# A third of seven block products split into seven: the experts' first layer of a gated cross-attention block

## The chip, the cores and the metric

The kernel runs on one core of a Trainium2 chip. A core has five engines that run their own instruction queues and meet through semaphores: TensorE (PE; matmuls, into the eight PSUM banks), VectorE (DVE), ScalarE (ACT), GpSimd (POOL) and SyncE (SP; here it only issues DMAs). Weight loads for TensorE are shown as an engine of their own, PEld. The metric is the device time of one execution in microseconds (us). Everything is float32; a matmul instruction of the program appears in the trace as two records.

## The reference

A gated block over 4096 tokens of 512 features, with a context of 3202 rows:

```python
x = x + jnp.tanh(g_xattn[0]) * _L0_xattn_ref(_layernorm(x), ctx_1024, w_sim, b_sim, W_qv, b_qv)
x = x + jnp.tanh(g_ffn[0]) * _L0_ffn_ref(_layernorm(x), w_router, b_router, w1, b1, w2, b2)
```

The first part is a cross-attention. The second part, the one that is touched here, is a mixture of 8 experts: each token goes to its two best experts, an expert has 640 places, and

```python
buf = zeros((e, cap, d)).at[e_flat, posc].add(where(keep[:, None], xf[tok], 0.0))     # e=8, cap=640, d=512
h = gelu(einsum('ecd,edf->ecf', buf, w1) + b1[:, None, :], approximate=False)          # f=2048
out = einsum('ecf,efd->ecd', h, w2) + b2[:, None, :]
```

after which the rows are weighted by the gates and added back to their tokens.

## The kernel before

The attention comes first (lines up to about 1600), then routing (`s2`), then one loop over the 8 experts (`for e in range(E)`), which is the part that matters here. An expert takes about 120 us: a first, hidden layer of some 59 us and an output layer of some 61 us.

**The hidden layer.** It works feature-major: `hT[p, l, idx, t]` holds 128 features by 640 tokens per (l, idx). The layer runs over `idx` = 0 to 7, called blocks here; a block makes two groups of 128 features, `lo` (l = 0) and `hi` (l = 1). Its weights are a 2x2 of pieces (two halves of the 512 inputs, lo and hi), its tokens a 2x2 as well (two halves of the inputs, two halves of the 640 tokens, `HC` = 320). So a block is a 2x2 by 2x2 matrix product, and it is done with seven products in place of eight (Strassen in Winograd's form). The sums of the weights come from `w1_sums` (line 1646, VectorE, written into the spare tiles `w1s` or over a piece of the weights), the sums of the tokens from `x_forms` (line 2068). A product (`product`, line 2273, in `hidden`, line 2256) is two matmul instructions, 128 features by 320 tokens, with 256 inputs. The products are numbered as in the code:

- 0 goes to bank X; ScalarE copies X to Y (line 2301)
- 3 goes to bank Q; ScalarE copies Q to `p5` in SBUF (L2305)
- 4 is added onto Y; ScalarE copies Y to Z (L2310)
- 1 is added onto X; ScalarE applies gelu to X: first half of lo (L2315); VectorE: second half of lo is Y + p5 (L2318, or L2332)
- 5 is added onto Z; ScalarE copies Z to the first half of hi, or to bank W (L2327); VectorE: second half of hi is Z + p5 (L2328)
- 6 is added onto Y and 2 onto W, in blocks 6 and 7 alone; elsewhere they are split.

**The split of products 2 and 6.** For two neighbouring blocks, called a pair (0 to 3), the same product of both is a matrix product of 256 features, 256 inputs and 320 tokens, again a 2x2 by 2x2 of pieces (128 x 128 by 128 x 160). For products 2 and 6 of pairs 0 to 2 `parts` (line 2216) does it with seven sub-products of one matmul instruction each, 160 tokens wide, which `hidden` lays between the products of one later block (1 to 6) in three steps (`first`, `second`, `third`). Its operands are made by `deep_w` (L2210 to L2213) and `deep_x` (L2197 to L2200), its partial results lie in a PSUM tile of three slots from the pool `ps_tr` (tag "tr", two tiles used in turn, also by the transposes) and in half a bank, moved on by two small copies (L2234, L2238), and four VectorE additions put them onto `hT` (L2246 to L2249).

**The order.** The order on each engine is written out by hand: `chained(eng, op)` puts an operation behind the last one given for that engine (`mm`, `dv`, `ac`, `ld`). The order of the program is therefore the order of each queue. Gelus whose input is not ready are put on a list, `owed`, and laid in by `due(n)` at given places of the next block. The semaphore waits follow from the data, a PSUM or SBUF tile that is used again waits for the last reader of what it held before. GpSimd does almost nothing here but issue indirect DMAs: five gathers of the output rows at an expert's start (L2435) and five scatters at its end (L2508), the gathers waiting until the scatters of the expert before have landed. Expert 0 has some of its first products done ahead (`early`) and is otherwise alike.

**The output layer** uses the sets of tiles `sets[0]` and `sets[1]`, and `u2` and `p7`, for the operands of its own two-level products (`inner`, `deep`, `plain`); `p5s` and the operands of the hidden layer's split lie in the same tiles while these are free.

Of the kernel before, what the change touches and what calls it, by code (L numbers as in the profile page):

```python
# [9 lines left out]
ALU = mybir.AluOpType  # L10
# [10 lines left out]
def gated_layer(ctx, tc, x, x_t, ctxt, ctxt_t, ctxt_c, ctxt_r, g_xattn, g_ffn, w_sim, w_sim_r, b_sim, W_qv, W_qv_t, b_qv, b_qv_c, w_router, b_router, w1, b1, w2, b2, out):  # L21
# [1974 lines left out]
    with ExitStack() as s3:  # L1996
# [20 lines left out]
        def dv(*ops):  # L2017
            return chained("dv", *ops)

        def ac(*ops):  # L2020
            return chained("ac", *ops)

        def ld(*ops):
            return chained("ld", *ops)
# [149 lines left out]
        def rows_of(ti, s):  # L2174
# [9 lines left out]
            k: (b, [flat_set[i][:, q * HH : (q + 1) * HH] for q in range(3)] + [p7[:, i - 5, :HH]])  # L2184
            for k, i, b in (("2", 5, xT[2]), ("6", 6, B22))
        }

        def w_of(k, pair):
            n = 3 * (2 * (pair % 2) + (k == "6"))
            return [flat_set[2 + (n + q) // 4][:, (n + q) % 4 * P : ((n + q) % 4 + 1) * P] for q in range(3)]  # L2190

        def deep_x(k):

            b, (t1, t2, t4, t3) = x_of[k]
            b11, b12, b21, b22 = (b[:, c, d : d + HH] for c in range(2) for d in (0, HH))
            return [
                lambda: tt(t1, b12, b11, ALU.subtract),  # L2197
                lambda: tt(t2, b22, t1, ALU.subtract),
                lambda: tt(t3, b22, b12, ALU.subtract),
                lambda: tt(t4, b21, t2, ALU.subtract),  # L2200
            ]

        def deep_w(e, k, pair):

            a = w1_forms(e, pair // 2)[int(k)]
            f = pair % 2 * 2 * P
            a11, a12, a21, a22 = (a[:, c, f + r : f + r + P] for r in (0, P) for c in range(2))
            s1, s2, s4 = w_of(k, pair)
            return [
                lambda: tt(s1, a21, a22, ALU.add),  # L2210
                lambda: tt(s2, s1, a11, ALU.subtract),
                lambda: tt(a21, a11, a21, ALU.subtract),
                lambda: tt(s4, a12, s2, ALU.subtract),  # L2213
            ]

        def parts(e, k, pair, c_bank):

            XWQ = ps_tr.tile([P, DC, P], F32, name=f"d{e}_{k}{pair}", tag="tr").rearrange("p c t -> p (c t)")
            X, W, Q = (XWQ[:, i * HH : (i + 1) * HH] for i in range(3))
            YZ = banks[c_bank][:, : 2 * HH]  # L2220
            Y, Z = YZ[:, :HH], YZ[:, HH:]
            a = w1_forms(e, pair // 2)[int(k)]
            f = pair % 2 * 2 * P
            a11, a12, s3, a22 = (a[:, c, f + r : f + r + P] for r in (0, P) for c in range(2))
            s1, s2, s4 = w_of(k, pair)
            b, (t1, t2, t4, t3) = x_of[k]
            b11, _, b21, b22 = (b[:, c, d : d + HH] for c in range(2) for d in (0, HH))
            dst = hT[:, 0, 2 * pair : 2 * pair + 2, HC:] if k == "6" else hT[:, 1, 2 * pair : 2 * pair + 2, :HC]

            def first():  # L2230
                mm(X, a11, b11, True, True)
                mm(Q, s1, t1, False, True)
                mm(W, a22, t4, False, True)
                ac(lambda: nc.scalar.copy(Y, X))  # L2234

            def second():
                mm(Y, s2, t2, False, True)
                ac(lambda: nc.scalar.copy(Z, Y))  # L2238
                mm(X, a12, b21, False, True)

            def third():
                mm(Z, s3, t3, False, True)
                mm(Y, s4, b22, False, True)

            adds = [
                lambda: tt(dst[:, :, HH:], dst[:, :, HH:], Q.unsqueeze(1).to_broadcast([P, 2, HH]), ALU.add),  # L2246
                lambda: tt(dst[:, :, :HH], dst[:, :, :HH], XWQ[:, : 2 * HH].rearrange("p (f t) -> p f t", f=2), ALU.add),
                lambda: tt(dst[:, 0, HH:], dst[:, 0, HH:], Y, ALU.add),
                lambda: tt(  # L2249
                    dst[:, 1, :].rearrange("p (d t) -> p d t", d=2), dst[:, 1, :].rearrange("p (d t) -> p d t", d=2),  # L2250
                    Z.unsqueeze(1).to_broadcast([P, 2, HH]), ALU.add,
                ),
            ]
            return first, second, third, adds, dst

        def hidden(e, idx):

# [11 lines left out]
            if 1 <= idx <= DEEP_IDX:  # L2269
                k, pair = ("6", idx // 2) if idx % 2 else ("2", idx // 2 - 1)  # L2270
                part = parts(e, k, pair, 5 if split else 2 + (idx + 1) % 2)

            def product(ps, k, start=False):
                for i in range(2):
                    mm(ps, A[k][i], XS[{2: 6, 6: 2}.get(k, k)][i], start and i == 0, i == 1)

            def step(i):
                if part:
                    part[i]()

            def due(n):
                ac(*owed[:n])
                del owed[:n]

            if there and idx:
                ac(lambda: nc.scalar.copy(Y, early.pop(f)))  # L2286
                step(0)
                product(Y, 4)
                due(1)
                ac(lambda: nc.scalar.copy(Z, Y))  # L2290
                step(1)
                product(Q, 3, True)
                ac(lambda: nc.scalar.copy(p5, Q))
                step(2)
                due(1)
            else:
                if there:
                    ac(lambda: nc.scalar.copy(Y, early.pop(f)))
                else:
                    product(X, 0, True)  # L2300
                    ac(lambda: nc.scalar.copy(Y, X))
                step(0)
                due(1)
                product(Q, 3, True)
                ac(lambda: nc.scalar.copy(p5, Q))  # L2305
                step(1)
                if not part:
                    due(1)
                product(Y, 4)
                ac(lambda: nc.scalar.copy(Z, Y))  # L2310
                step(2)
                due(1)
            if not there:
                product(X, 1)
                ac(lambda: nc.scalar.activation(lo[:, :HC], X, AF.Gelu, bias=b_lo))  # L2315
            due(len(owed))
            if split:
                dv(lambda: tt(lo[:, HC:], Y, p5, ALU.add))  # L2318
# [108 lines left out]
        for e in range(E):  # L2427
# [2 lines left out]
                ld(lambda: load_w2(e, 0), lambda: load_w2(e, 1))  # L2430
            b2_t = sb.tile([P, D], F32, name=f"b2_{e}", tag="b2", bufs=1)
            ld(lambda: nc.sync.dma_start(b2_t, b2[e].partition_broadcast(P)))
            cf, ti = cf_of[e], ti_of[e]
            for s in range(NST):
                gather = nc.gpsimd.indirect_dma_start(  # L2435
# [12 lines left out]

            (B11w, B12w, B21w, B22w), right, inner = output(e)
            bias = [add(s, slice(None), b2_t) for s in range(NST)]  # L2450
            dv(*deep_w(e, "6", 0), *deep_x("6"))
            if e:
                dv(*w1_sums(e, 0, 2))
            for idx in range(2 * KQ):
                if more and idx == 2:
                    ld(*[lambda s=s: rows_in(e + 1, s) for s in range(NST - 1)])
# [6 lines left out]
                    dv(*deep_w(e, "2", 0), *deep_x("2"))  # L2463
                if idx in (1, 3):
                    dv(*deep_w(e, "6", 1 + idx // 2), *deep_w(e, "2", 1 + idx // 2))
                if idx in (4, 6, 7):
                    k = (0, 2, 4)[(4, 6, 7).index(idx)]
                    dv(left(1, k, k + 2), left(3, k, k + 2))
# [175 lines left out]
```

## Time and profile before

| | us |
|---|---|
| median of 3 runs (2552.12 to 2552.47) | 2552.36 |
| the profiled execution, its own time | 2551.32 |
| its span, first to last instruction | 2549.5 |
| one expert, from a point of the chain to the same point of the next (1630.15 to 1750.20) | 120.05 |
| hidden layer of expert 1 (1704.70 to 1763.50) | 58.80 |
| one product, from starts (four records of 320) | 1.077 |

In the profile's timelines each row has its start and its duration in us, the engine, the source line, the operation, the tiles written and read (buffer numbers left out), the shapes and the number of instructions merged; in brackets is the time that the engine was idle before, and what ended it. All matmuls of the expert stage have line L2027, the helper that issues them; `d` is a PSUM tile of the split, `bank` a bank, `l` a tile of `sets`, `w` and `w1s` weights and their sums. The records of TensorE overlap: their starts are measured, their ends modelled. In a table of stretches the columns are busy time and number of instructions of PE, PEld, DVE, ACT and POOL, then the granted TensorE clock, the DMA share and GB/s.

### The profile page before, as it was taken

To read this page: it belongs to the slowest core of one execution; us is meant where nothing else is said; L and a number is where in the kernel's file an instruction comes from. 1 tells how busy PE (TensorE), PEld (TensorE's weight loads), DVE (VectorE), ACT (ScalarE), POOL (GpSimd) and SP (SyncE) were. 2 spreads that over 40 slices of the span, in tenths; PEclk is the share of its full clock that TensorE was granted. 3 is DMA by queue.
4 is the path that set the end of the run, shared out by engine and by line. 5 is a ranking of instruction groups with operands and counts; after the bars stand their busy time and mean duration, and the time that the engine had idled before them with its cause. 6 is when DMAs were issued, how large, how long until landed. Compare 5 with 4: busy or idle time off the path is not lost.

```text
span 2549.5 us, 37831 instructions
## 1 busy us (share of the span) xinstructions
PE 2531.7 (99%) x14256; PEld 2214.7 (87%) x14256; DVE 1974.8 (77%) x4118; ACT 715.8 (28%) x1556; POOL 275.5 (11%) x399
## 2 busy tenths in 40 slices
PE   9999999999999999999999999999999999999998
PEld 7788888998988988989989887798888888888978
DVE  8887865876967868859658657887888888787877
ACT  1112302323123123123231144424232332424150
POOL 0101220001001000000000056010101010101010
PEclk9999999999999999999999999999999999999999
DMA  7568795875976957758748895322313141414120
GB/s 265 194 215 295 268 350 175 281 266 167 317 226 205 307 194 241 265 188 285 249 154 292 272 353 190 130 100 95 133 67 133 71 156 43 162 42 158 47 103 21
DMA packets 198407, 489.08 MB, mean 192 GB/s; under 512 B 22462, under 2 KB 79102, under 8 KB 196176
## 3 DMA queue, kind: packets, MB, share of 16 engines
q1 hardware_dynamic: 151984, 386.37, 45.0%
q0 software_dynamic: 21696, 59.07, 6.4%
q10 hardware_dynamic: 24544, 41.21, 4.4%
q8 instruction: 113, 1.85, 0.3%
q14 instruction: 70, 0.57, 0.1%
HBM read 397.40 MB, written 97.52 MB: 194 GB/s over the span
## 4 chain that ended last, share of the span: by engine, by line
PE 89%; issue 5%; DVE 4%; POOL 1%; DMA 1%; ACT 0%; POOLq 0%; SPq 0%; DVEq 0%
PE bank L2027 30%; PE bank L761 21%; PE bank L984 13%; PE bank L1153 6%; PE bank L1510 5%; PE x1p L1755 2%; PE bank L1254 2%; PE d L2027 2%; PE p7d L1510 1%; PE p4d L1510 1%; PE bank L813 1%; PE v L1254 1%; PE bps L2103 1%; DVE SM L1023 1%; PE bank L990 1%
## 5 line engine op out<-in xcount | busy, mean ns | idle before, releaser
L761 PE MATMUL bank<-Qp,kt 128*128 128x256 f32 x1344 | 305.2, 379 | 0.0
L761 PEld LDWEIGHTS bank<-Qp,kt 128*128 128x128 f32 x1344 | 254.4, 190 | 34.1
L2027 PE MATMUL bank<-w,hT 128*128 128x256 f32 (+1 forms) x1280 | 260.7, 359 | 0.7 <-ACT u L2519 0.7
L2027 PEld LDWEIGHTS bank<-w,hT 128*128 128x128 f32 x1280 | 223.8, 190 | 27.4 <-ACT u L2519 1.1
L761 PE MATMUL bank<-q,kt 128*128 128x256 f32 x1008 | 231.3, 379 | 0.0
L761 PEld LDWEIGHTS bank<-q,kt 128*128 128x128 f32 x1008 | 191.5, 190 | 26.0
L2027 PE MATMUL bank<-bT,w 128*128 128x320 f32 x736 | 211.1, 432 | 0.6 <-ACT bank L2310 0.6
L984 PE MATMUL bank<-dt,vf 128*128 128x128 f32 x1680 | 204.8, 275 | 0.0
L984 PEld LDWEIGHTS bank<-dt,vf 128*128 128x128 f32 x1680 | 196.0, 192 | 0.0
L2027 PEld LDWEIGHTS bank<-bT,w 128*128 128x128 f32 x736 | 136.6, 190 | 50.5 <-ACT bank L2310 1.1
L2027 PE MATMUL bank<-XT,w1s 128*128 128x320 f32 x512 | 156.4, 433 | 0.1
L804 DVE TENSOR_TENSOR M<-M,E_all 128x1024 f32<-128x1024 f32 x80 | 97.9, 1223 | 46.0 <-ACT E_all L721 44.6
L2508 POOL DMA_INDIRECT out<-acc,ti x40 | 39.7, 992 | 806.7 <-DVE acc L2447 800.0
L1755 PE MATMUL x1p<-W,q2T 128*128 128x264 f32 x512 | 117.7, 391 | 3.0 <-DVE lg L1777 1.8
L717 DVE TENSOR_TENSOR E_all<-bank,p5s 128x512 f32<-128x512 f32 x42 | 28.9, 688 | 113.4 <-ACT bank L716 113.3
L1755 PEld LDWEIGHTS x1p<-W,q2T 128*128 128x128 f32 x512 | 97.7, 192 | 20.1 <-PE pos L1871 1.8
L2027 PEld LDWEIGHTS bank<-XT,w1s 128*128 128x128 f32 x512 | 91.9, 190 | 25.9 <-ACT bank L2286 0.5
L891 DVE TENSOR_TENSOR E_all<-E_all,mb 128x1024 f32<-128x1024 f32 x84 | 101.2, 1211 | 10.3 <-ACT mb L866 10.3
L984 PE MATMUL bank<-E_all,vf 128*128 128x128 f32 x828 | 106.5, 275 | 0.0
L892 ACT ACTIVATE E_all<-E_all 128x1024 f32<-128x1024 f32 x84 | 88.8, 1057 | 49.8 <-DVE E_all L891 49.3
L984 PEld LDWEIGHTS bank<-E_all,vf 128*128 128x128 f32 x828 | 99.8, 192 | 0.3
L2027 PEld LDWEIGHTS bank<-l,l 128*128 128x128 f32 x736 | 92.9, 192 | 7.6
(644 smaller groups left out, 4955.1 us busy)
## 6 DMA issues: line engine op xcount, KB each, us to landing
vf<-vf_d SPq DMA_DIRECT2D x122, 768.0 KB
kt<-kt_d SPq DMA_DIRECT2D x84, 512.0 KB
w<-in_w SPq DMA_DIRECT2D x16, 2048.0 KB
w<-in_w SPq DMA_DIRECT2D x32, 1024.0 KB
kt<-in_ctxt_t SPq DMA_DIRECT2D x84, 384.0 KB
wp<-wt_d SPq DMA_DIRECT2D x56, 520.0 KB
buf_d<-zero SPq DMA_DIRECT2D x80, 129.0 KB
xb<-buf_d SPq DMA_DIRECT2D x39, 258.0 KB
```

The lines of the kernel that those rows point to most:

```text
L717: tt(dst(1, 1), Z, p5, ALU.add)
L761: nc.tensor.matmul(ps[:, jl, :], kts[j][:, KSLOT[p], k, :], B[p][:, k, :], start=start and jl == 0 and k == 0, stop=stop and k == 1, skip_ ...
L804: tt(M, M, e[:, :, h], ALU.max)
L891: live[g]["last"] = tt(e, e, m, ALU.subtract)
L892: live[g]["exp"] = nc.scalar.activation(e, e, AF.Exp)
L984: nc.tensor.matmul(ps, a[:, j, :], rhs[r][:, j, :], start=start and j == 0, stop=j == NP - 1 and (rest is None or add is None), skip_group ...
L1153: nc.tensor.matmul(ps[b], vt[:, j - i * JH, b * P : (b + 1) * P], right(j) if j < NJ else right_c, start=start and j == 0 and b == 0, stop ...
L1254: mm = nc.tensor.matmul(acc[k][:, b, :], a[:, b * P : (b + 1) * P], r, start=start and b == 0, stop=stop, skip_group_check=True,)
L1510: nc.tensor.matmul(ps[m], A[p][:, k, m * P : (m + 1) * P], wt[:, k, :], start=start and k == 0, stop=stop and k == DC - 1, skip_group_chec ...
L1755: mm = nc.tensor.matmul(ps[:, j, :B1], qTs[g][:, c, q * P : (q + 1) * P], W1[:, c, j, :], start=(c == 0), stop=(c == DC - 1))
L2027: return chained("pe", lambda: nc.tensor.matmul(ps, a, b, start=start, stop=stop, skip_group_check=True))
L2508: sc = nc.gpsimd.indirect_dma_start(out=out[:, :], out_offset=rows_of(ti, s), in_=accs[s][:, :], in_offset=None, bounds_check=N - 1, oob_i ...
```

## The change

For pairs 1, 2 and 3 (in expert 0: 2 and 3), product 3 of the two blocks is also split into seven sub-products. In a block where that holds (`triple`), products are issued without product 3 and without its copy to `p5`; in the even block of the pair, `parts(e, "3", ...)` is laid in (`extra`), ahead of the split of products 2 or 6 at each of the three steps. Its results are copied into both `p5s` tiles by three ScalarE copies (`copies`) and completed by two VectorE additions; the odd block then uses the second of them. The steps of the splits move: step 1 comes after product 4 and step 2 after product 1. Of the places where owed gelus are laid in, two are left out in a `triple` block, so that what is owed beyond one comes after the gelu of product 1.

The operands of the new split are made by GpSimd, four sums of 128x160 per expert (`deep_x("3")`) and four of 128x128 per pair (`third_w`), in tiles of `sets[0]` and in `u2`. The first eight of them stand in GpSimd's queue ahead of the expert's gathers; the lines that make VectorE's sums there are moved up with them. The other fours follow blocks 3 and 5.

```diff
+        flat_low = [t.rearrange("p a b -> p (a b)") for t in sets[0]]
+        x_of["3"] = (xT[0], [flat_low[6][:, q * HH : (q + 1) * HH] for q in range(3)] + [u2[:, 0, :HH]])
+
+        def third_split(e, idx):
+            return idx >= (KQ if e == 0 else 2)
 
         def w_of(k, pair):
+            if k == "3":
+                return [flat_low[4 + pair % 2][:, q * P : (q + 1) * P] for q in range(3)]
...
-        def deep_x(k):
+        def deep_x(k, tt=tt):
...
-        def deep_w(e, k, pair):
+        def deep_w(e, k, pair, tt=tt):
...
-            X, W, Q = (XWQ[:, i * HH : (i + 1) * HH] for i in range(3))
+            X, W, Q = (XWQ[:, i * HH : (i + 1) * HH] for i in ((2, 0, 1) if k == "3" else (0, 1, 2)))
...
+            def copies():
+                nc.scalar.copy(p5s[1], XWQ[:, : 2 * HH])
+                nc.scalar.copy(p5s[0][:, :HH], X)
+                return nc.scalar.copy(p5s[0][:, HH:], Q)
+
             adds = [
+                lambda: tt(p5s[0][:, HH:], p5s[0][:, HH:], Y, ALU.add),
+                lambda: tt(
+                    p5s[1].rearrange("p (d t) -> p d t", d=2), p5s[1].rearrange("p (d t) -> p d t", d=2),
+                    Z.unsqueeze(1).to_broadcast([P, 2, HH]), ALU.add,
+                ),
+            ] if k == "3" else [
...
+            triple = third_split(e, idx)
+            extra = parts(e, "3", idx // 2, 1) if triple and idx % 2 == 0 else None
...
             def step(i):
+                if extra:
+                    extra[i]()
                 if part:
                     part[i]()
...
                 step(0)
                 due(1)
-                product(Q, 3, True)
-                ac(lambda: nc.scalar.copy(p5, Q))
-                step(1)
-                if not part:
-                    due(1)
+                if not triple:
+                    product(Q, 3, True)
+                    ac(lambda: nc.scalar.copy(p5, Q))
+                    step(1)
+                    if not part:
+                        due(1)
                 product(Y, 4)
                 ac(lambda: nc.scalar.copy(Z, Y))
-                step(2)
-                due(1)
+                step(1 if triple else 2)
+                if not triple:
+                    due(1)
             if not there:
                 product(X, 1)
                 ac(lambda: nc.scalar.activation(lo[:, :HC], X, AF.Gelu, bias=b_lo))
+            if triple:
+                step(2)
+            if extra:
+                ac(extra[5])
+                dv(*extra[3])
             due(len(owed))
...
+            dv(*deep_w(e, "6", 0), *deep_x("6"))
+            if e:
+                dv(*w1_sums(e, 0, 2))
+
+            def third_w(pair):
+                return chained("gp", *deep_w(e, "3", pair, nc.gpsimd.tensor_tensor))
+
+            chained("gp", *deep_x("3", nc.gpsimd.tensor_tensor))
+            if third_split(e, 2):
+                third_w(1)
             cf, ti = cf_of[e], ti_of[e]
...
-            dv(*deep_w(e, "6", 0), *deep_x("6"))
-            if e:
-                dv(*w1_sums(e, 0, 2))
             for idx in range(2 * KQ):
...
+                if idx in (3, 5):
+                    third_w(1 + idx // 2)
```

More of the change, by code (lines that the diff above doesn't have):

```diff
@@ L2227, in parts @@
             b11, _, b21, b22 = (b[:, c, d : d + HH] for c in range(2) for d in (0, HH))
[L2228 removed]
+            dst = None if k == "3" else hT[:, 0, 2 * pair : 2 * pair + 2, HC:] if k == "6" else hT[:, 1, 2 * pair : 2 * pair + 2, :HC]
             def first():
@@ L2253, in parts @@
             ]
-            return first, second, third, adds, dst
+            return first, second, third, adds, dst, copies
         def hidden(e, idx):
```

## The prediction

> **What bounds the kernel now.** I read the engines' shares and the chain that ended last first, then the stretch table over one hidden layer, then the timelines of TensorE and ScalarE inside it, since the change lies there alone.
>
> ```profile
> PE 2531.7 (99%) x14256; PEld 2214.7 (87%) x14256; DVE 1974.8 (77%) x4118; ACT 715.8 (28%) x1556; POOL 275.5 (11%) x399
> PE 89%; issue 5%; DVE 4%; POOL 1%; DMA 1%; ACT 0%; POOLq 0%; SPq 0%; DVEq 0%
> 1704.70:1763.50 58.80, 58.80 (x262) 44.78 (x261) 42.90 (x113) 30.82 (x75) 7.12 (x7) 1.00 0.44 161
> ```
>
> The third line is expert 1's hidden layer: 58.80 us long, TensorE (the figure after the comma) busy for all of it at clock 1.00, VectorE 42.90, ScalarE 30.82, GpSimd 7.12. TensorE alone is the limit, so time comes only from fewer matmul columns, and goes wherever TensorE is made to wait.
>
> TensorE in blocks 1 to 3:
>
> ```profile
> 1711.18 0.43 PE L2027 MATMUL d<-bT,w1s 128*128 128x160 f32 x2
> ...
> 1715.23 3.39 PE L2027 MATMUL bank<-bT,w 128*128 128x320 f32 x12
> 1718.46 0.43 PE L2027 MATMUL d<-XT,w 128*128 128x160 f32 x2
> 1718.73 0.43 PE L2027 MATMUL d<-l,l 128*128 128x160 f32 x2
> ...
> 1733.03 0.43 PE L2027 MATMUL d<-XT,w 128*128 128x160 f32 x2
> ```
>
> Starts give the true rate, ends are modelled. Twelve records of 320 columns take 1718.46 - 1715.23 = 3.23 us; a product is four, so 1.077 us (its last record is drawn to 1.24). A block takes (1733.03 - 1711.18)/3 = 7.283 us; less five products that leaves 1.90 for its seven sub-products (two records of 160 each): 0.271 each.
>
> Block 7, the last, has no split pair; TensorE, then ScalarE:
>
> ```profile
> 1755.96 1.24 PE L2027 MATMUL bank<-bT,w 128*128 128x320 f32 x4
> 1757.04 2.32 PE L2027 MATMUL bank<-XT,w1s 128*128 128x320 f32 x8
> 1759.19 2.32 PE L2027 MATMUL bank<-bT,w 128*128 128x320 f32 x8
> 1762.42 1.28 PE L2027 MATMUL bank<-XT,w 128*128 128x320 f32 x4
> 1763.54 0.81 PE L2027 MATMUL bank<-w,hT 128*128 128x256 f32 x3
> ```
> ```profile
> 1757.24 0.41 ACT L2301 COPY bank<-bank 128x320 f32<-128x320 f32 x1 [2.82 <-PE bank L2027]
> 1758.69 0.56 ACT L2325 ACTIVATE hT<-hT,b_t 128x320 f32<-128x320 f32 x1
> 1759.72 0.56 ACT L2325 ACTIVATE hT<-hT,b_t 128x320 f32<-128x320 f32 x1
> 1760.47 0.53 ACT L2315 ACTIVATE hT<-bank,b_t 128x320 f32<-128x320 f32 x1 [0.19 <-PE bank L2027]
> 1760.90 0.55 ACT L2335 ACTIVATE hT<-hT,b_t 128x320 f32<-128x320 f32 x1
> 1761.35 0.52 ACT L2336 ACTIVATE hT<-bank,b_t 128x320 f32<-128x320 f32 x1
> 1761.90 0.41 ACT L2327 COPY bank<-bank 128x320 f32<-128x320 f32 x1
> ```
> ```profile
> PEld bank L2027 <- ACT bank L2327: 2.2, 8, 0.3
> 2491.57 0.70 PE L2027 MATMUL bank<-w,hT 128*128 128x256 f32 x2 [0.68 <-ACT u L2519]
> ```
>
> The reader is to see three things. The copy of product 0 starts 0.04 after the product's drawn end (1755.96 + 1.24) and is hidden behind product 3. The copy to W, which product 2 needs, ends at 1762.31, just ahead of product 2 at 1762.42, and the weight loads already wait for it in all 8 experts: block 7 has no slack on ScalarE. And what a bare copy costs: in the last expert TensorE stood idle 0.68 behind a copy that lasts 0.59, so 0.09 more than the copy.
>
> **The change part by part.** The sum is made against the profiled execution's 2551.32 us; the median is 1.04 above it. Pairs of blocks changed: expert 0 two, the seven others three, 23 in all.
>
> Matmuls. Per pair, two products of 1.077 go and seven sub-products of 0.271 come: 2.153 - 1.900 = 0.253 us. Times 23: **-5.8**.
>
> Block 7, first bubble. Without product 3 nothing stands between product 0 and product 4, and product 4 adds onto the copy of product 0. TensorE could go on 1.077 after product 0's start; it may go on at 1.24 + 0.41 + 0.09 = 1.74. Bubble 0.66, times 8 experts: **+5.3**.
>
> Block 7, second bubble. Five activations are owed when it begins. Before, three were laid between the products; now one is, and four stand between the gelu of product 1 (L2315) and the copy to W. From block start: product 4 at 1.74, product 1 at 2.81, its gelu at 2.81 + 1.28 = 4.09; the next activation 0.43 later (1760.47 to 1760.90), the further three 0.45 apart (1760.90 to 1761.35), the copy 0.55 after the last (1761.35 to 1761.90): 6.42; TensorE goes on 0.41 + 0.05 later, 6.88. It wants product 2 at 2.81 + 3 x 1.077 = 6.04. Bubble 0.84, less 0.04 that is lost there already (1763.54 - 1762.42 against 1.077): 0.80, times 8: **+6.4**. The hi addition and later steps follow the W copy as before, so no more is lost behind it.
>
> A buffer that comes free late. An even changed block now takes two of the two PSUM tiles for sub-products, so the next block's split must wait until VectorE has read the even block's own one. Even block, from its start: product 0 to 1.08, two triples of sub-products to 2.70, product 4 to 3.78, four to 4.87, product 1 to 5.94, four to 7.02, product 5 to 8.10; the odd block's first sub-product is wanted at 9.18. ScalarE: gelu of product 1 at 6.14, then the three new copies at 6.57, 6.89 and 7.08 (0.43, 0.32 and 0.19 apart, as 320- and 160-column copies are in the trace), the last done at 7.37. VectorE, which ends block 1's work 4.5 us into block 2 (at 1721.9) and then idles: the two new additions at 7.39 and 7.62, the lo addition at 8.02, the split's first two at 8.42 and 8.82 (0.23 and 0.40 apart, as at 1723.82 and 1722.62), the second done at 9.30; TensorE goes on at 9.34. Wait 0.16, in blocks 3 (seven experts) and 5 (eight): **+2.4**. Block 7 takes no such tile.
>
> GpSimd's sums: 32 of 128x160 and 92 of 128x128. No row shows a two-input sum of this size there. Nearest: a one-input 128x128 operation, 0.295 us; the far end, the 128x512 fill, 0.56. Each queue that they pass: ahead of the gathers stand 8 of them for an expert (4 in the first), but the gathers wait for the scatters to land until 1715.40 anyway, while the scatters were issued by 1706.9: 8 fit at up to 1.0 us. The first user, block 2, is at 1718.46; if an operation took over 1.4 us, TensorE would wait for them. The later two groups of four follow the gathers and are wanted 7 us on; the scatters at the expert's end come after them. So their own time is costed at nothing. What they may cost is VectorE: if the two engines get in each other's way, four operations delay VectorE by 0 to 4 x 0.56. Its additions for block 3's split end 1.19 before block 4 wants that tile, and block 5's 1.0 before block 6. Taking turns at 0.295, 1.18 is lost: 0 in block 4, 0.18 in block 6, times 8: **+1.4**, which I take as the nearest row gives it; ends 0 and, at 0.56, 7 x 1.05 + 8 x 1.24 = 17. A gain is excluded: these sums are new work. At the expert's start VectorE has 2.3 us in hand ahead of block 1's split (its last operand is done at 1708.85 and wanted at 1711.18) against 4 such operations.
>
> The Trainium skill speaks against this part (SBUF — State Buffer, "Who interferes with whom"): a VectorE operation with two SBUF inputs and a GpSimd operation that reads SBUF exclude each other for a whole instruction, and which goes first decides. No row of this trace shows it. GPSIMD Engine Reference ("Elementwise — side-by-side cycle accounting") has 4497 ns for 2048 elements, an estimated 0.28 us for 128: by that four turns cost 1.1 and this term would be 0.8 instead.
>
> Costed at nothing: the two additions a pair on VectorE (0.23 + 0.40 beside 15.9 us that it idles in this layer; their lateness is counted above); three more small ScalarE copies a pair outside block 7 (28 us idle); the moved VectorE sums, which keep their place on that engine because only GpSimd's gathers stood between. If that cover went, TensorE would wait at the next copy, at 0.4 each.
>
> Sum: -5.8 + 5.3 + 6.4 + 2.4 + 1.4 = +9.7: 2561.0 for the profiled execution, **2562** against the median.
>
> **The rivals.**
> The saving comes whole, and the kernel is faster: the mechanism is that block 7's copies stay hidden because they start before the drawn ends, which are modelled. It gives 2552.4 - 5.8 = 2546.6. For it: seven blocks an expert show no wait on such a copy. Against: the 0.68 row is a wait on just such a copy. It decides where both bubbles together are under (5.8 - 2.4)/8 = 0.43 us, against 1.46 here.
> The tile wait and the port cost nothing and the second bubble is half as long (activations closer together when they stand in a row): -5.8 + 5.3 + 3.2 = +2.7, 2555. Against: 0.45 is the spacing of two that do stand in a row.
> VectorE and GpSimd block each other fully: 4 x 0.45 = 1.8 lost per group, 7 x 0.6 + 8 x 0.8 = 10.6 in place of 1.4: 2571. For it: VectorE runs without a gap just where the sums become ready (the S1 sum at 1718.45 and after). Against: it idles 3 us before each block's late additions, where GpSimd can catch up if VectorE goes first.
>
> **How the numbers follow.** No change to be told from noise is within 0.2%, 5.1 us. Forecast 0.65, the whole saving 0.05, the small loss 0.11, the blocked port 0.19. The forecast's own range is 2558 to 2566: the bubbles 0.15 either way per expert (1.2), the tile wait 0 to 0.3 (2.4 down, 2.1 up). The range, 2556 to 2570, cuts about half of the small loss, all of the faster case and the upper part of the blocked port. Faster 0.05, same 0.11, slower 0.84.
>
> **What would show it.** In an expert with three pairs 24 matmul records of 320 columns go and 42 of 160 come. Product 4 of block 7 starts 1.7 after product 0, and its product 2 about 0.8 late behind L2327's copy; in blocks 3 and 5 the first sub-product waits 0.1 to 0.2 for a VectorE addition; GpSimd's sums show 0.3 to 0.5 us each. An expert's period, 120.05 before (1630.15 to 1750.20), should be 121.3. The prediction is wrong if block 7 shows no idle TensorE, or if TensorE waits for GpSimd in block 2.

## The result, and the profile after

The changed kernel takes 2562.8 us in the median (2562.31 to 2563.99, six runs), the kernel before 2552.24 beside it (2551.55 to 2554.75, six runs): a ratio of 1.0044, with a 95% interval of 1.0033 to 1.0054. It is slower by 10.6 us. The profiled execution took 2562.84 us with a span of 2561.1.

The engines' shares and the chain that ended last, after:

```profile
PE 2532.4 (99%) x14394; PEld 2223.6 (87%) x14394; DVE 2006.3 (78%) x4164; ACT 723.8 (28%) x1625; POOL 357.1 (14%) x523
PE 89%; DVE 4%; issue 4%; ACT 1%; POOL 1%; DMA 1%; another core or an unknown queue 0%; POOLq 0%; SPq 0%; DVEq 0%
```

TensorE has 138 records more, 6 for each of the 23 pairs (14 of 160 columns in place of 8 of 320). GpSimd's busy time grew by 82 us, and ScalarE has 1% of the chain where it had 0%. That 1% is block 7. TensorE in block 7 of expert 1, after:

```profile
1760.11 1.24 PE L2027 MATMUL bank<-bT,w 128*128 128x320 f32 x4
1761.85 1.34 PE L2027 MATMUL bank<-XT,w1s 128*128 128x320 f32 x4 [0.50 <-ACT bank L2324]
1763.03 2.32 PE L2027 MATMUL bank<-bT,w 128*128 128x320 f32 x8
1765.19 1.24 PE L2027 MATMUL bank<-bT,w1s 128*128 128x320 f32 x4
1767.10 1.34 PE L2027 MATMUL bank<-XT,w 128*128 128x320 f32 x4 [0.67 <-ACT bank L2357]
1768.28 7.07 PE L2027 MATMUL bank<-w,hT 128*128 128x256 f32 x32
```

Product 4 starts 1.74 after product 0 (1761.85 - 1760.11) instead of 1.077. Product 2 starts 1.91 after product 6 (1767.10 - 1765.19). Behind both waits the product takes 1.18 to the next start (1763.03 - 1761.85, 1768.28 - 1767.10): 0.10 more than one in full flow, and this is drawn as 1.34 instead of 1.24. The queue of ScalarE in the same block:

```profile
1764.31 0.53 ACT L2340 ACTIVATE hT<-bank,b_t 128x320 f32<-128x320 f32 x1 [0.67 <-PE bank L2027]
1764.74 1.00 ACT L2355 ACTIVATE hT<-hT,b_t 128x320 f32<-128x320 f32 x2
1765.64 0.55 ACT L2365 ACTIVATE hT<-hT,b_t 128x320 f32<-128x320 f32 x1
1766.09 0.51 ACT L2366 ACTIVATE hT<-bank,b_t 128x320 f32<-128x320 f32 x1
1766.63 0.41 ACT L2357 COPY bank<-bank 128x320 f32<-128x320 f32 x1
```

The gelu of product 1 (L2340) is followed by four owed activations without a gap, and the copy that product 2 needs (L2357; it was L2327 before) comes only then. Over the whole expert stage the waits of TensorE (total, times, longest) are:

```profile
PE bank L2027 <- ACT bank L2357: 5.4, 8, 0.7
PE bank L2027 <- ACT bank L2324: 4.0, 8, 0.5
PE d L2027 <- DVE l L2204: 2.0, 1, 2.0
```

Eight waits for each of the two copies, one per expert, and one long wait for VectorE in expert 0, which the prediction had not spoken of. Before, TensorE was idle for 0.95 at that place (1595.52, with no releaser named in that profile). Where the prediction had expected the tile wait, in block 3, there is none; TensorE, then VectorE:

```profile
1728.25 2.32 PE L2027 MATMUL bank<-bT,w 128*128 128x320 f32 x8
1730.40 0.43 PE L2027 MATMUL d<-bT,w1s 128*128 128x160 f32 x2
```
```profile
1729.66 0.48 DVE L2264 TENSOR_TENSOR hT<-hT,d 128x320 f32<-128x320 f32 x1
1730.05 0.48 DVE L2265 TENSOR_TENSOR hT<-hT,d 128x320 f32<-128x320 f32 x1
```

The first sub-product starts at 1730.40, exactly two products behind 1728.25 and so without any wait, while the addition that was to hold it up (L2265) still runs until 1730.53.

Below, "stage" is the time from the first sub-product of expert 0's block 1 to the end of the span (before: 2549.5 - 1594.14 = 955.4; after: 2561.1 - 1593.75 = 967.4), and "period" the time from one expert to the next (before 120.05; after 121.25 for the first five experts and 121.00 for the others). The stage grew by 12.0 us.

### The profile page after: what moved, and what is told of

Read it like the earlier page. It is cut to its first block, busy times and chain, and to the rows that moved or that the text cites. A ratio compares the mean times of both kernels' runs of the same rounds, so it can differ in the third digit from the quotient of the medians.

```text
span 2561.1 us, 38523 instructions
## 1 busy us (share of the span) xinstructions
PE 2532.4 (99%) x14394; PEld 2223.6 (87%) x14394; DVE 2006.3 (78%) x4164; ACT 723.8 (28%) x1625; POOL 357.1 (14%) x523
## 4 chain that ended last, share of the span: by engine, by line
PE 89%; DVE 4%; issue 4%; ACT 1%; POOL 1%; DMA 1%; another core or an unknown queue 0%; POOLq 0%; SPq 0%; DVEq 0%
PE bank L2027 30%; PE bank L761 21%; PE bank L984 13%; PE bank L1153 6%; PE bank L1510 5%; PE d L2027 3%; PE bank L1254 2%; PE x1p L1755 2%; PE p7d L1510 1%; PE p4d L1510 1%; PE bank L813 1%; PE v L1254 1%; PE bps L2103 1%; DVE SM L1023 1%; PE bank L990 1%
## 5 line engine op out<-in xcount | busy, mean ns | idle before, releaser
L2027 PE MATMUL bank<-bT,w 128*128 128x320 f32 x736 | 217.3, 432 | 0.6 <-ACT bank L2334 0.6
L2027 PE MATMUL bank<-l,l 128*128 128x128 f32 (+1 forms) x782 | 109.2, 280 | 0.0
L2027 PEld LDWEIGHTS bank<-l,l 128*128 128x128 f32 x782 | 100.7, 192 | 7.8 <-issue 0.4
L2027 PE MATMUL bank<-XT,w1s 128*128 128x320 f32 x328 | 102.7, 440 | 4.1 <-ACT bank L2324 4.0
```

What stands on the lines that cost most here:

```text
L2027: return chained("pe", lambda: nc.tensor.matmul(ps, a, b, start=start, stop=stop, skip_group_check=True))
```

## The experiments

The kernel before runs beside every group of experiments. It took 2551.89 beside the first four and 2545.2 to 2545.6 beside the rest, where the expert stage of the experiments' kernels also begins 6 to 8 us earlier (1588 instead of 1594 to 1596); what a kernel costs is therefore always its distance to the kernel before of the same group. Intervals are 95%.

### Block 7: the two bubbles one by one, and together

The second bubble is undone by laying the owed activations in again: two at step 0 in block 7, and one behind product 4 wherever no split of products 2 and 6 is laid in.

```diff
-                due(1)
+                due(2 if triple and not part else 1)
...
-                if not triple:
+                if not (triple and part):
                     due(1)
```

> Only the places of ScalarE's owed activations in block 7 are changed: two behind the copy of product 0 and one behind the copy of product 4, where one and none were; two are left ahead of the copy to W in place of four. Theory A (the second bubble of block 7 is the order of ScalarE's queue): the wait behind the copy to W goes, 0.83 us and the 0.10 by which the first matmul after a wait is longer, less the 0.04 that the kernel before loses there too, 8 times: -7.1, 2555.7 us. The first bubble (0.66) stays. Theory B (the loss is GpSimd's sums slowing VectorE, and a wait taken away at one place comes back at the next): under 2 us gained, 2561 or more.

Measured: 2555.23 us (2554.01 to 2556.28), 1.0012 of before (1.0003 to 1.0021), +3.3 us. The waits for L2357 are gone, those for L2324 stay at 4.0.

The first bubble is undone by issuing product 0 of block 7, with its copy, already in block 6, ahead of that block's product 2.

```diff
-                else:
+                elif idx < KF - 1:
                     product(X, 0, True)
                     ac(lambda: nc.scalar.copy(Y, X))
...
+                if idx == KF - 2:
+                    for i in range(2):
+                        mm(X, w1_forms(e, h)[0][:, i, (f + 1) * P : (f + 2) * P], XS[0][i], i == 0, i == 1)
+                    ac(lambda: nc.scalar.copy(banks[3][:, :HC], X))
                 product(W, 2)
```

> Only product 0 of block 7 and its copy are moved: ahead of block 6's product 2, so that this product covers the copy. Theory A: the first bubble goes, 0.66 + 0.10, 8 times: -6.1, 2556.7 us; the second bubble stays at 0.83, since ScalarE's queue behind it is the same. Theory B: under 2 us gained.

Measured: 2556.2 us (2553.49 to 2558.78), 1.0015 (1.0006 to 1.0024), +4.3. The waits for L2324 are gone, those for L2357 stay at 5.4.

Both edits together:

> The two edits together. Theory A: they add up, -13.2, 2549.6 us: 2.7 under the kernel before (2552.3), because the saved matmuls (5.8) outweigh what is left, some 4 us that VectorE loses to GpSimd's sums at the start of expert 0 and at the end of the output layers. TensorE shows no wait in block 7. Theory B: 2560 or more.

Measured: 2549.33 us (2546.72 to 2552.83), 0.9990 (0.9981 to 0.9999), -2.6. Block 7 of expert 1 in the timeline of TensorE of this kernel (product 0 has gone ahead, so product 4 comes first):

```profile
1760.14 1.24 PE L2027 MATMUL bank<-XT,w1s 128*128 128x320 f32 x4
1761.21 2.32 PE L2027 MATMUL bank<-bT,w 128*128 128x320 f32 x8
1763.37 1.24 PE L2027 MATMUL bank<-bT,w1s 128*128 128x320 f32 x4
1764.44 1.28 PE L2027 MATMUL bank<-XT,w 128*128 128x320 f32 x4
```

Starts lie 1.07 to 1.08 apart for each product: no wait is left. The same can be had by leaving pair 3 alone, so that block 7 keeps product 3:

```diff
-            return idx >= (KQ if e == 0 else 2)
+            return (KQ if e == 0 else 2) <= idx < DEEP_IDX
...
-                if idx in (3, 5):
+                if idx == 3:
                     third_w(1 + idx // 2)
```

> Product 3 is split for pairs 1 and 2 only (expert 0: pair 2), so blocks 6 and 7 are as in the kernel before. Theory A: both bubbles go (-13.2) and 8 of 23 pairs' savings with them (+2.0): 2551.6 us, about the time before; the savings of 15 pairs are 3.8 and the losses to GpSimd's sums about 4. Theory B (GpSimd's sums are the loss): a third of it goes with a third of the sums, 2559 or more.

Measured: 2551.56 us (2550.03 to 2554.05), ratio 1.000 (0.9991 to 1.0009), -0.3. All four came out within 0.5 us of what the first theory gave. So block 7 is worth 10.6 + 2.6 = 13.2 us by medians. The profile gives the same: 0.66 + 0.83 + 2 x 0.10, less the 0.04 that was lost before, is 1.65 us an expert, 13.2 for eight. The first theory is shown: the loss lies in block 7, in two parts that can be taken away separately, and the saving of the matmuls is real.

### GpSimd's sums, first try: make them later

The four 128x160 sums of each expert go later: behind the fourth scatter of the expert before, in expert 0 behind its gathers.

```diff
-            chained("gp", *deep_x("3", nc.gpsimd.tensor_tensor))
-            if third_split(e, 2):
+            if e:
+                with tc.issue_after(stored[-1]):
+                    tail["gp"] = deep_x("3", nc.gpsimd.tensor_tensor)[0]()
+                chained("gp", *deep_x("3", nc.gpsimd.tensor_tensor)[1:])
                 third_w(1)
...
+                if idx == 1 and not e:
+                    with tc.issue_after(gather.ins):
+                        tail["gp"] = deep_x("3", nc.gpsimd.tensor_tensor)[0]()
+                    chained("gp", *deep_x("3", nc.gpsimd.tensor_tensor)[1:])
```

> Only the place of GpSimd's first sums is changed: in expert 0 the four token sums come behind its gathers, in the other experts the token sums behind the fourth of the five scatters and the first four weight sums ahead of the gathers. Theory A (in expert 0 GpSimd's sums slow the VectorE sums that TensorE waits for in block 1, and in the later experts they slow the output layer's last additions): the wait of 2.0 us in expert 0's block 1 falls to the 0.95 of the kernel before (-1.1, and up to -1.7 more where the clock fell after the long wait), and the 0.28 us that 5 output layers lose goes (-1.3): 2559 to 2560.5 us from 2562.8. Rival: VectorE is slowed wherever the sums stand, and the loss moves to block 2: 2562 to 2563, with a new TensorE wait there.

Measured: 2553.33 us (2552.75 to 2554.76), 1.0031 (1.0019 to 1.0043), +7.8 over before; stage 963.3, all periods 121.00. Both amounts fit the expectation, and for a while that looked like the answer. It was not all of it, as the last experiments show: this kernel and the changed one did not run side by side.

Or VectorE makes all the sums:

```diff
-                return chained("gp", *deep_w(e, "3", pair, nc.gpsimd.tensor_tensor))
+                return chained("dv", *deep_w(e, "3", pair))
...
+                if idx == 1 and not e:
+                    chained("dv", *deep_x("3"))
+                if idx in (2, 4):
+                    third_w(1 + idx // 2)
```

> The same sums, all made by VectorE: the first eight behind its own sums at an expert's start, the others behind the weight sums of blocks 2 and 4; expert 0's token sums after block 1. VectorE gets 0.20 to 0.24 us for each, 3.5 us an expert. Theory A (VectorE has room in the hidden layer; what GpSimd costs is the length of VectorE's operations beside its own): the same gain as with the sums moved, 2559 to 2560.5 us, and VectorE's weight sums back at 0.42. Rival (VectorE has no room, which is why GpSimd is used): the additions of blocks 3 and 5 come late, TensorE waits for them in blocks 4 and 6, 2564 or more.

Measured: 2554.74 us (2553.0 to 2554.88), 1.0036 (1.0023 to 1.0050), +9.2; stage 963.0, period 120.88, and no wait of TensorE for VectorE in blocks 2 to 6. The period is 0.12 below that with GpSimd's sums. A new wait of 0.4 for a copy (L2241) stands once in the whole stage. So VectorE has room for the sums, but the median gains less than theory A gave. The profiled run, from which the stage is read, is the fastest of the five (2553.0); the others took 2554.6 to 2554.9, and no trace shows why.

What the two engines do to each other is plain in the changed kernel, where the rows of VectorE, then of GpSimd, overlap:

```profile
1732.27 0.68 DVE L1654 TENSOR_TENSOR w<-w 128x256 f32<-128x256 f32 x1
1732.88 0.67 DVE L1655 TENSOR_TENSOR w1s<-w,w1s 128x256 f32<-128x256 f32 x1
1733.47 1.47 DVE L2394 TENSOR_TENSOR TX<-w 128x1024 f32<-128x1024 f32 x1
```
```profile
1732.75 0.52 POOL L2218 TENSOR_TENSOR l<-l,w1s 128x128 f32<-128x128 f32 x1
1733.23 0.63 POOL L2219 TENSOR_TENSOR w1s<-w1s 128x128 f32<-128x128 f32 x1
1733.83 1.44 POOL L2220 TENSOR_TENSOR l<-w1s,l 128x128 f32<-128x128 f32 x1
```

The first two of VectorE last 0.42 before and 0.42 with all sums on VectorE, the third 1.22; so an overlap costs VectorE about 0.25 each time. GpSimd's sum of 128x128 lasts 0.45 where VectorE is quiet, and up to 1.44 beside it. The rows look like turns taken operation by operation. Each sum ends 0.31 to 0.33 after the VectorE operation that was running when it began: L2218 at 1733.27 after L1654 at 1732.95, L2219 at 1733.86 after L1655 at 1733.55, L2220 at 1735.27 after L2394 at 1734.94. And the VectorE operation that comes next is the one that is longer by 0.25.

### The tile that was not waited for

The compiled order explains block 3. The odd block's split takes, of the two PSUM tiles, the one that came free first, and that is the new split's, which only ScalarE's copies read. Its first sub-product waits for ScalarE and TensorE, not for VectorE:

```
L2027 Matmult d_62_10537<-bT,w1s_8596 128x160 [waits PE_49,Activation_49]
```

To test it, each kind of split gets its own tile, so that the odd block must take the one that VectorE reads (two more lines, not shown, let the transposes take the two tiles in turn):

```diff
-            XWQ = ps_tr.tile([P, DC, P], F32, name=f"d{e}_{k}{pair}", tag="tr").rearrange("p c t -> p (c t)")
+            XWQ = ps_tr.tile([P, DC, P], F32, name=f"d{e}_{k}{pair}", tag="tr1" if k == "3" else "tr0", bufs=1).rearrange("p c t -> p (c t)")
```

> The two PSUM tiles of the splits are given out by kind: one for products 2 and 6, the other for product 3 (the transposes still take them in turn). The prediction's term for a buffer that comes free late rested on the odd block's split taking the tile of the even block's split of product 2; the trace after shows no wait there. Theory A (it was the wrong tile, and the reading of VectorE's queue was right): with this assignment TensorE waits for a VectorE addition at the first sub-product of blocks 3 and 5, 0.15 to 0.2 us, and 0.1 more for the first matmul behind it: +2.4 to +4.5, 2565 to 2567 us. Rival (VectorE's additions are done earlier than worked out): no wait, 2562.8.

Measured: 2561.86 us (2560.27 to 2562.11), 1.0063 (1.0049 to 1.0077), +16.3, where the changed kernel costs +10.6 in the result and +9.6 in the pair further down; the period is 121.71, 0.71 above 121.00. TensorE, then VectorE, of this kernel:

```profile
1723.20 2.32 PE L2027 MATMUL bank<-bT,w 128*128 128x320 f32 x8
1725.63 0.51 PE L2027 MATMUL d<-bT,w1s 128*128 128x160 f32 x2
1725.98 0.43 PE L2027 MATMUL d<-l,l 128*128 128x160 f32 x2
```
```profile
1725.01 0.48 DVE L2265 TENSOR_TENSOR hT<-hT,d 128x320 f32<-128x320 f32 x1
```

Now the sub-product, wanted at 1725.36, starts at 1725.63, 0.14 behind the end of L2265 (1725.49), and takes 0.08 longer than the usual 0.27: 0.35 in all, in two blocks of an expert, which is the 0.71; 15 such blocks make 5.3, and the stage is 5.9 longer than the changed kernel's in that pair (971.7 against 965.8); the rest are two more such waits, in blocks 2 and 3 of expert 0, at 0.3 each. That is more than the 2.4 to 4.5 of theory A, whose wait of 0.15 to 0.2 was too short. The mechanism of the prediction is real, but the change does not meet it.

### Everything repaired

Both edits of block 7 and the late sums:

> The two repairs of block 7 and the moved first sums together. Theory A: the gains add up: 2549.3 less 2.3 to 4.0, so 2545.3 to 2547.0 us, 0.2 to 0.27% under the kernel before. Rival: 2549 or more, if the sums cost as much in their new places.

Measured: 2540.07 us (2538.96 to 2541.76), 0.9979 (0.9970 to 0.9988), -5.5; period 119.36. Theory A is borne out by the distance to the kernel before (4.9 to 6.6 less); its times in us were reckoned from the first group, where the kernel before takes 6 us more.

Both edits of block 7, with all the sums on VectorE:

> Both repairs of block 7, as in the run of both, and all sums of the new split on VectorE, none on GpSimd. Theory A (VectorE has room for them: with the sums on VectorE alone TensorE waited for VectorE nowhere in blocks 4 and 6, and that kernel lay 9.2 above before where the late GpSimd sums lay 7.8): 13.3 less than the 9.2, so 4.1 faster than before, ratio 0.998 to 0.999, a period of 119.3, no wait for L2324 or L2357. Rival B (GpSimd is needed: with block 7 no longer giving VectorE 1.65 us an expert to catch up, its additions come late to the tiles and TensorE waits for L2264 or L2265): at 0.2 to 1.0 us an expert, 2 to 4 us slower than the best kernel with the late sums, about level with before.

Measured: 2539.52 us (2538.99 to 2541.89), 0.9978 (0.9968 to 0.9988), -5.9; period 119.22, no wait for either copy and none for VectorE from block 2 on. Rival B is refuted, and the gain is larger than theory A gave by the +9.2. The page of this kernel:

```profile
PE 2523.8 (99%) x14394; PEld 2222.2 (88%) x14394; DVE 2012.7 (79%) x4288; ACT 723.7 (29%) x1625; POOL 276.4 (11%) x399
```

It has TensorE's 14394 records and GpSimd's 399 instructions of before. Of the period of before, 120.05, 3 x 0.253 = 0.76 goes with the matmuls and 0.06 with the late copy that the last experiments speak of; that leaves 119.23, against 119.22 measured. So the whole saving that the matmuls promise is had, and GpSimd isn't needed for it.

### Where GpSimd's sums cost time: expert 0 alone, and a pair on one chip

Only expert 0's four sums move, to behind its gathers; the seven other experts keep theirs.

> Only the four 128x160 sums of expert 0 move, behind its gathers; the seven other experts keep theirs where the change put them. Theory A (GpSimd costs time at two separate places: expert 0's start, and the end of the output layers of experts 0 to 4): the wait for VectorE in expert 0's block 1 goes back from 2.03 to 0.95 and the clock stays at 1.00 behind it, while the periods stay at 121.25 for the first experts and 121.00 for the last. The stage becomes 1.1 (the wait alone) to 2.8 (wait and lowered clock) shorter than the changed kernel's 967.35, so 964.5 to 966.3, and the median lies 7.8 to 9.5 above the kernel before on the same chip, where the change itself lay 10.6 above. Rival B (the lowered clock has nothing to do with the longer wait): a clock under 0.8 between the start of expert 0's block 1 and 8 us later is seen in spite of a wait of 0.95. Rival C (the output layers' loss follows from expert 0): all periods are 121.0 and the median lies under 8 above before.

Measured: 2553.11 us (2552.5 to 2554.64), 1.0030 (1.0019 to 1.0041), +7.7; stage 963.3, the wait back at 0.94, clock 1.00 behind it, and all periods 121.00. Theory A falls in its second half: the output layers' loss is gone although the sums stand there as in the changed kernel. Neither can it well follow from expert 0 (rival C), since the two programs have the same order on every engine from expert 1 on. What is left is where, or when, the program ran. The copy behind which TensorE loses time there is late in the kernel before too. ScalarE at the end of expert 0's output layer, in the kernel before, then in the changed kernel, then in this one:

```profile
1701.63 0.25 ACT L2408 COPY bank<-bank 128x128 f32<-128x128 f32 x1 [1.89 <-PE bank L2027]
```
```profile
1705.46 0.25 ACT L2438 COPY bank<-bank 128x128 f32<-128x128 f32 x1 [2.06 <-PE bank L2027]
```
```profile
1696.43 0.25 ACT L2438 COPY bank<-bank 128x128 f32<-128x128 f32 x1 [1.54 <-PE bank L2027]
```

It is idle 1.54 where the copy is on time, so 0.35 late before and 0.52 late after. A pair run side by side on one chip tells it apart: the changed kernel again, and the late sums again.

> The changed kernel itself, beside the next one on one chip. What is open is the 0.25 us that TensorE loses at the end of the output layers of experts 0 to 4 behind a late ScalarE copy (L2438). Theory A (the sums that GpSimd makes there delay it): this kernel has periods of 121.25 in the first five experts wherever it runs, and the kernel with the late sums has 121.00 on the same chip. Rival B (it belongs to the chip: the copy is 0.35 late in the kernel before too, on the chip of its profile, and was not late in six kernels on two other chips, of which two kept the sums where the change put them): both kernels of this pair have the loss, or neither has. In expert 0 both theories expect the wait for VectorE at 2.03 here and 0.95 in the other; whether the clock falls behind the wait of 2.03 is open. Medians: this one 1.1 to 2.8 above the other by expert 0 alone, and by theory A another 1.3.

> The kernel with GpSimd's sums late in every expert, beside the changed kernel on one chip. Theory A: periods of 121.00 throughout, whatever the other one shows. Rival B: the same periods as the other one, expert by expert, with 121.25 if the chip is one on which that copy is late. Median 1.1 to 2.8 (rival B) or 2.4 to 4.1 (theory A) below the changed kernel's, and 7.5 to 9.5 above the kernel before.

Measured: the changed kernel 2554.78 us (2553.4 to 2555.59), 1.0035 (1.0021 to 1.0049), +9.6; the late sums 2553.2 us (2552.5 to 2554.97), 1.0033 (1.0021 to 1.0045), +8.0, 1.6 less. Both have periods of 121.00 in every expert, the changed kernel in spite of its long wait in expert 0: rival B, and rival C of the run before falls. The sums alone don't cause the loss at the output layers' end. But neither does a chip's number tell where it is met: the record has chip 10 for this pair and for the first four experiments too, and there the run of both edits has the 0.25 in most of its periods (119.34 to 119.61). The loss came to 5 x 0.25 in the changed kernel's first profile and to 7 x 0.06 in that of before, so 0.8 of the 12.0. Why the copy is late there, and whether the sums make it 0.52 late rather than 0.35, was not found.

What GpSimd's early sums do cost lies in expert 0. TensorE in the changed kernel of this pair, then with the late sums:

```profile
1587.99 0.43 PE L2027 MATMUL d<-bT,w1s 128*128 128x160 f32 x2
1590.44 0.56 PE L2027 MATMUL d<-l,l 128*128 128x160 f32 x2 [2.02 <-DVE l L2204]
1591.96 2.34 PE L2027 MATMUL bank<-XT,w1s 128*128 128x320 f32 x4
```
```profile
1588.05 0.44 PE L2027 MATMUL d<-bT,w1s 128*128 128x160 f32 x2
1589.42 0.54 PE L2027 MATMUL d<-l,l 128*128 128x160 f32 x2 [0.94 <-DVE l L2204]
1590.62 1.24 PE L2027 MATMUL bank<-XT,w1s 128*128 128x320 f32 x4
```

The wait is 1.08 longer. In the first profile after, VectorE's rows just ahead of it, then GpSimd's, show why:

```profile
1590.04 1.15 DVE L2074 TENSOR_TENSOR bT<-bT 128x640 f32<-128x640 f32 x1
1591.11 1.14 DVE L2075 TENSOR_TENSOR XT<-bT,XT 128x640 f32<-128x640 f32 x1
```
```profile
1589.40 1.11 POOL L2204 TENSOR_TENSOR l<-XT 128x160 f32<-128x160 f32 x1 [5.00 <-PE bank L2116]
1590.58 0.98 POOL L2205 TENSOR_TENSOR l<-XT,l 128x160 f32<-128x160 f32 x1
1591.53 1.10 POOL L2206 TENSOR_TENSOR u<-XT 128x160 f32<-128x160 f32 x1
```

L2074 and L2075 last 0.82 each without GpSimd beside them. They stand in VectorE's queue ahead of the sums that TensorE waits for, and so do L2092 and L2094, of which the first ones last 0.41 and 0.38 here and 0.15 and 0.22 with the late sums: 0.33 + 0.32 + 0.26 + 0.16 make 1.07 of the 1.08. Behind the longer wait, products also run slower: in the table of stretches of the pair, the granted clock (the number after GpSimd's column) is 0.50 in the changed kernel and 1.00 with the late sums:

```profile
1591.00:1593.00 2.00, 1.73 (x5) 1.37 (x5) 1.97 (x8) 0.74 (x2) 1.39 (x3) 0.50 1.04 374
```
```profile
1591.00:1593.00 2.00, 2.00 (x11) 1.58 (x10) 1.93 (x8) 1.24 (x4) 1.70 (x2) 1.00 1.08 356
```

From the end of the wait to the product after next TensorE needs 4.27 (1590.44 to 1594.71) against 2.82 (1589.42 to 1592.24): 1.45 more. Of seven profiles with the wait of 2.0, four have such a stretch and three have none, so in the medians it counts for part of that.

## Why the prediction was right

The forecast was +9.7 us; the two measurements of the changed kernel are +10.6 and +9.6. The main mechanism, two bubbles in block 7 that outweigh the saving, is shown by the four experiments on block 7. But that the sum came out so close is partly luck: three errors nearly cancelled. Term by term:

- **Matmuls, -5.8.** Right. With everything else repaired the kernel is 5.9 us faster than before, and the period falls by what 3 x 0.253 asks.
- **Block 7, first bubble, +5.3, and second, +6.4.** The places, the releasing copies and the lengths were right: product 4 at 1.74 after product 0, as forecast, and product 2 late by 0.83 against 0.84. Mis-sized is what follows a bubble: the first product behind a wait takes 0.10 more. That was to be read in the trace of before, where a product behind a wait is drawn with 1.34 instead of 1.24. The two together measured 13.2 instead of 11.7.
- **A buffer that comes free late, +2.4.** This step failed: the cost is 0. The prediction took the two tiles as used in strict turn; the odd block's split gets the one that was released first, the new split's. The times of VectorE were right (second addition forecast 8.82 after the block's start, measured 8.84), and with the other tile the wait is there, at 0.35 instead of 0.16.
- **GpSimd's sums beside VectorE, +1.4 in block 6.** The price was right: taking turns at 0.295 a sum was forecast, and 0.25 to 0.33 was measured. The place was wrong. Block 6 loses nothing, since the tile that was first in line there is again the other one. The time goes in expert 0, where the prediction spoke only of the 2.3 us in hand of the other experts and overlooked that TensorE already stood idle there in the profile of before (0.95): there nothing was in hand. It costs 1.1 for the wait, 0 to 1.5 for the lowered clock, and 0.12 in each period (121.00 against 120.88 with the sums on VectorE), 1.0 for eight experts, whose place was not followed further: 2.1 to 3.6 in all. GpSimd's queue was also not as the change and the prediction have it: of the eight first sums only five run ahead of the gathers. L2218 to L2220 come behind the second gather (in expert 1 at 1721.51 to 1722.79, the gathers L2475 at 1719.13 and 1720.47), and TensorE waits for none of them. The sums themselves were forecast at 0.3 to 0.5 us; they last 0.45 undisturbed, and in the mean of experts 1 to 7 between 0.50 and 0.95 by line.
- **Not foreseen at all:** 0.8 from the late copy in the output layers, met in the first profile after and not in the pair; what causes it is open.

Measured terms: -5.8 + 13.2 + 0 + 1.1 + 1.0 = +9.5, and up to 1.5 for the clock: 9.5 to 11.0 against +9.6 where the copy is on time. With the 0.8 of the late copy, and 1.5 for the clock that is lowered in that profile, they make 11.8 of the 12.0 by which the stage grew.

The rivals: that the saving comes whole needed bubbles under 0.43, and they are 1.65. The small loss needed activations closer than 0.45, and they stand 0.43 to 0.54 apart. The blocked port at 0.45 a sum did not come: VectorE loses 0.25 to 0.33 for a sum that itself lasts 0.45 to 0.52, and no time in blocks 4 and 6. The rule of the Trainium skill (SBUF — State Buffer, "Who interferes with whom"), a lock for a whole instruction, isn't refuted by that. The rows fit it: a sum is over only 0.31 to 0.33 after the VectorE operation that it met has ended (hence up to 1.44), and the next VectorE operation is longer by the 0.25. Only the turn of a sum is shorter than the sum as the profile draws it. (In the prediction's sentence on the other page, four turns of 0.28 come to 1.12, so that its 0.8 should be 1.0; nothing rests on it.)

## What to carry to other kernels

A product that is taken out takes its cover with it: before one is removed or split, list the copies that ran behind it and where the work now falls that was laid in around it. Here both repairs were a matter of order and turned a loss of 0.4% into a gain of 0.1%, and of 0.2% once the new split's sums were moved as well. And where a forecast depends on which of several buffers a step gets, or on slack at one point of a loop, look that up for the first pass of the loop as well and in the compiled order, not by the rule of thumb.

## What the runs showed of the hardware

- The granted clock fell to 0.50 for 3.41 us (1590.83 to 1594.24 in the pair's changed kernel) behind a wait of 2.0 us in four of seven profiles, and never behind the wait of 0.95. The Trainium skill (TensorE: Matmul & The Clock Gate, "Part 1: The HAM clock gate") gives about 3.4 us of idleness, counted in windows that run freely, for a fall to one half. The 0.50 and the 3.41 agree with it, but TensorE was idle for only 2.0 us at a stretch: in the 3.41 us that ended with the fall it was busy for 1.40 (1.2 to 1.5 in the four profiles). A free-running window would fit a fall in only some runs: in the kernel with two pairs the clock falls at 1510.71 and at 1599.45, 26 times 3.413 apart, and when the same steps are counted from the earlier fall of the three profiles without one here, the wait lies across two steps, busy for 1.6 to 2.8 each. No threshold follows: in the run of both edits the clock also fell at 1557.21, behind 3.41 us of which 2.03 were busy.
- A VectorE operation of two inputs in SBUF that had a GpSimd sum ahead of it grew by 0.25 to 0.33 us (0.42 to 0.68, 1.22 to 1.47, 0.82 to 1.15). A GpSimd sum that met a running one ended 0.31 to 0.33 us behind it (128x128), and so grew from 0.45 to as much as 1.44.
- The same program was 7 to 8 us faster in some groups of runs than in others (before: 2552.24 and 2545.21; changed: 2562.8 and 2554.78), 5.8 of it ahead of the expert stage (which begins at 1593.75 and 1587.99 in the changed kernel's two profiles); the change's own cost was nearly the same, +10.6 and +9.6. The chip's number doesn't tell the groups apart: before took 2551.89 and 2545.21 on runs that both bear the number 10.
